# Where VectorE makes the token weights of a routed expert layer: early in its queue, or behind each tile's own gate product

## The chip, the cores and the metric

The kernel runs on one core of a Trainium2 chip, in float32 for everything that matters here. The metric is device microseconds (us) of one execution. The core has five engines with a queue each: TensorE (PE in the profile, its weight loads PEld), VectorE (DVE), ScalarE (ACT), GpSimd (POOL) and SyncE (SP). Each takes its instructions strictly in the order of its queue. DMAs are issued from SP's queue (plain ones) and from POOL's queue (indirect ones, which gather or scatter rows by a list of indices).

## The reference, cut to what matters

The program is a chain of four blocks over 2048 tokens of 128 features: an attention block with a gated feed-forward part, a routed expert layer (call it layer m), a slot-attention block, and a second routed expert layer (layer n). The change touches layer m alone:

```
shared_out = _expert(x, sg, su, sd)                 # silu(x @ sg.T) * (x @ su.T) @ sd.T
probs  = softmax(x @ wr.T + rb)                     # 7 routed experts
scores, idx = top_k(probs, 2);  scores = scores / scores.sum()
out = shared_out
for e in range(7):
    out = out + w[..., e:e + 1] * _expert(x, rg[e], ru[e], rd[e])   # w: scores at idx, else 0
```

So each token goes to two of seven experts, and each expert's result is multiplied by the token's weight for it, the "token weight" of the title.

## The kernel before, in words

Layer m sorts the 4096 pairs of token and expert by expert and cuts them into 38 tiles of at most 128 rows, one expert to a tile. Its steps, with the names and lines used below:

- **Shared expert.** `moe0_shared` (L1390) runs for four groups of 512 tokens. For each of three chunks it makes two products into PSUM (`gu`, L1397), a SiLU on ScalarE (`gss`, L1387) and the gate product on VectorE (`ma`, L1388); then 12 products, written as 24 matmuls in the profile, make `ym` (L603), and VectorE adds it to the residual `r` (L1402). `ym` lies in the pool `psX`, which has one buffer; the tiles' results `ynm` take the same buffer next, so the first tile cannot start before the last `r` addition has read `ym`.
- **Sorting.** `sort` (L1010) makes the lists: `frm` (which token rows a tile gathers), `to` (where its results go), and `sec` and `sgn` (L1105, L1106), which tell whether a row is its token's first or second choice. It also issues the first weight loads and gathers.
- **Gathers.** `fetch(j)` (L1257, DMA at L1264) gathers the 128 rows of tile j into `zs[j]`, each row 128 normalized features and one score. Two tiles share a buffer, and there are seven buffers, so 14 tiles fit. In the text F(j) is this gather on POOL's queue.
- **Weights.** `weights` (L1245, DMA at L1254, from SP's queue) loads the 576 KB of one tile's expert. There are six buffers; the load of tile j+6 waits for the last product of tile j.
- **Tile loop.** `tiles` (L1309). For tile j, TensorE does three gate products `gum` (L1410, six matmuls in the profile), the transposition of the next tile's rows (`turn`, L1316, copied to `zTn` by ScalarE at L1318), three more `gum`, and the down products of the tile before (`ynm`, L1421). ScalarE makes SiLU (`gsm`, L1387), VectorE the gate product (`am`, L1388), and ScalarE scales the result by the token weight on its way out of PSUM (`ysm`, L1425). `finish(j)` then issues the next weight load, the scatter of `ys` to `res` (L1325, R(j) in the text) and the next gather.
- **Token weight.** `moe0_down` (L1417) makes `wk[j]`, one number a row, from the score that came with the gather and from `sgn` and `sec` (L1419). It takes four buffers in turn, so wk(j) waits until `ysm` has used wk(j-4). It is also the last reader of `zs[j]` beside the transposition, so a gather into the same buffer waits for it.

The program is put in order by a scheduler that queues an instruction of an engine when it can be ready soonest by its own estimates; nothing in the source says where on VectorE's queue L1419 goes. As built, wk(0) stands in front of the addition of the third group's `ym`, wk(1), wk(2) and wk(3) stand behind it and in front of the last two `ma` of the shared expert, and from then on wk(j+4) stands between am(j+1) and am(j+2). On POOL's queue the built order is F(0) to F(15), R(0), then F F R R over and over, until the gathers are used up.

Of the kernel before, what the change touches and what calls it, by code (L numbers as in the profile page):

```python
# [15 lines left out]
ALU = mybir.AluOpType  # L16
# [5 lines left out]
D = 128  # L22
# [15 lines left out]
IP = 384  # L38
# [31 lines left out]
def pixart_kernel(  # L70
# [18 lines left out]
    V, S, G, PE = nc.vector, nc.scalar, nc.gpsimd, nc.tensor  # L89
# [768 lines left out]
    def wide(nm):  # L858
        return psS.tile([P, 512], F32, name=nm, tag="s")
# [524 lines left out]
    def silu_gate(a, gate, up, nm, n):  # L1384

        gs = ph.tile([P, 512], F32, name=f"gs{nm}", tag="gate2")[:, :n]
        S.activation(gs, gate, AF.Silu)  # L1387
        V.tensor_tensor(a, gs, up, ALU.mult)  # L1388

    def moe0_shared(R, i, zT):  # L1390
        g = R.b0 // 4 + i
        a = ph.tile([P, 3, 512], F32, name=f"ma{g}", tag="act")
        for c in range(3):
            ps = [wide(f"gu{g}_{c}_{j}") for j in range(2)]
            for j in range(2):
                w = j * IP + c * P
                PE.matmul(ps[j], lhsT=wsh[:, w : w + P], rhs=zT, start=True, stop=True)  # L1397
            silu_gate(a[:, c, :], ps[0], ps[1], f"s{g}_{c}", 512)
        y = psX.tile([P, 4, D], F32, name=f"ym{g}", tag="x")
        token_major(y, lambda c: a[:, c, :], lambda c: wsh[:, 2 * IP + c * D : 2 * IP + (c + 1) * D], 3)  # L1400
        rg = r[:, 4 * g : 4 * g + 4, :]
        V.tensor_tensor(rg, y, rg, ALU.add)  # L1402

    def moe0_up(w, zT, nm):
        ps = []
        for j in range(2):
            ps.append(wide(f"gu{nm}_{j}"))
            for c in range(3):
                k = j * IP + c * P
                PE.matmul(ps[j][:, c * P : (c + 1) * P], lhsT=w[:, k : k + P], rhs=zT, start=True, stop=True)  # L1410
            if j == 0:
                yield ps[0][:, IP:]
        a = ph.tile([P, IP], F32, name=f"a{nm}", tag="acts", bufs=3)
        silu_gate(a, ps[0][:, :IP], ps[1][:, :IP], nm, IP)
        yield a

    def moe0_down(w, a, y, ys, R, j):  # L1417
        wk = rt.tile([P, 1], F32, name=f"wk{j}", tag="wk", bufs=4)
        V.tensor_scalar(wk, R.zs[j][:, D : D + 1], R.sgn[:, j : j + 1], R.sec[:, j : j + 1], ALU.mult, ALU.add)  # L1419
        for c in range(3):  # L1420
            PE.matmul(  # L1421
                y, lhsT=a[:, c * P : (c + 1) * P], rhs=w[:, 2 * IP + c * D : 2 * IP + (c + 1) * D],
                start=(c == 0), stop=(c == 2),
            )
        S.activation(ys, y, AF.Copy, scale=wk)  # L1425
# [374 lines left out]
    for g in range(4):  # L1800
        moe0_shared(m0, g, zT[g])
    m0.tiles(moe0_up, moe0_down)
    slot_prologue()
    idle = wide("idle")
# [102 lines left out]
```

## Time and profile before

| | |
|---|---|
| time, median of 3 runs | 885.98 us (880.98 to 886.86) |
| the profiled execution | 882.33 us, of which span 880.6 us |
| mean granted TensorE clock | 0.955 of full speed |
| busy: PE, PEld | 783.8 us (89%), 623.0 us (71%) |
| busy: DVE, ACT, POOL | 548.8 us (62%), 411.7 us (47%), 358.9 us (41%) |
| moved by DMA | 65.18 MB, mean 74 GB/s |
| shared expert's last part and first gathers | about 484 to 507 us of the span |
| tile loop of layer m | about 507 to 614 us of the span |

Times in the views count from the first instruction of the span. In a timeline, a line gives start, duration, engine, source line, operation, output and inputs, how many instructions were merged, and in brackets how long the engine was idle before and what ended that. "issue" means that nothing the profile shows was waited for; "remote" that the wait was ended by something the profile cannot name. The ends of matmuls are modelled and not observed. POOL's rows for indirect DMAs show the issue, not the transfer.

### The profile page before, as it was taken

What the parts mean: (1) busy time and instruction counts of PE and PEld (TensorE: products, weight loads), DVE (VectorE), ACT (ScalarE), POOL (GpSimd) and SP (SyncE); (2) the same over time, 40 slices, a digit from 0 to 9 for tenths busy, and PEclk for the clock granted to TensorE, in tenths of its full rate; (3) what the DMA queues carried; (4) which work ended last, traced back from release to release, by engine and by line L of the source; (5) the groups of instructions that cost most, each with busy time, mean ns of one, the idle gap of its engine ahead of it and who ended that gap; (6) DMA issues with size and microseconds to landing.
All of it is one profiled execution on the core that took longest, in us unless ns stands there. A gap on an engine that the chain in (4) does not pass through costs nothing.

```text
span 880.6 us, 15517 instructions
## 1 busy us (share of the span) xinstructions
PE 783.8 (89%) x5469; PEld 623.0 (71%) x5469; DVE 548.8 (62%) x1748; ACT 411.7 (47%) x931; POOL 358.9 (41%) x457
## 2 busy tenths in 40 slices
PE   6999999999999999999899688789789898983776
PEld 4688887877678788765666478688476776673775
DVE  3687766765657776885879322232588799851333
ACT  3566767666654454443231023344486756231222
POOL 2234324241424333436430656654244445543565
PEclk9999999999999999999999889999989999956989
DMA  8200000001200000002002457774300000038873
GB/s 313 85 2 1 1 1 2 1 1 39 60 1 11 10 11 14 18 1 77 13 18 73 150 168 227 236 267 153 93 1 2 1 1 1 1 64 211 271 241 117
DMA packets 36529, 65.18 MB, mean 74 GB/s; under 512 B 4579, under 2 KB 25014, under 8 KB 35812
## 3 DMA queue, kind: packets, MB, share of 16 engines
q1 hardware_dynamic: 32179, 55.11, 20.4%
q0 software_dynamic: 4272, 9.09, 3.4%
q8 instruction: 43, 0.70, 0.3%
q14 instruction: 35, 0.28, 0.1%
HBM read 55.71 MB, written 8.93 MB: 73 GB/s over the span
## 4 chain that ended last, share of the span: by engine, by line
PE 73%; DVE 11%; issue 4%; ACT 4%; DMA 3%; POOL 3%; SPq 1%; another core or an unknown queue 1%; POOLq 0%; ACTq 0%; DVEq 0%
PE gum L1410 6%; PE pq L367 6%; PE ynm L1421 4%; PE pk L377 4%; PE te L524 3%; PE po L534 3%; PE s L471 3%; PE s L462 3%; PE ya L566 3%; PE pv L384 3%; PE pv L400 3%; PE ya L557 3%; PE h1n L1766 2%; PE idle L1526 2%; PE ynn L1776 2%
## 5 line engine op out<-in xcount | busy, mean ns | idle before, releaser
L509 POOL TENSOR_TENSOR e<-e,ri 128x1024 f32<-128x1024 f32 x32 | 61.0, 1909 | 143.4 <-DVE ri L495 130.3
L482 DVE TENSOR_REDUCE mx<-s 128x8 f32<-128x1024 f32 (+1 forms) x64 | 64.4, 1007 | 63.0 <-PE s L471 47.5
L494 DVE TENSOR_REDUCE ri<-e 128x8 f32<-128x1024 f32 (+1 forms) x64 | 63.7, 995 | 19.0 <-ACT e L490 18.3
L1410 PE MATMUL gum<-zTnm,wm 128*128 128x128 f32 x456 | 64.8, 285 | 11.8 <-ACT zTnm L1318 10.2
L503 POOL TENSOR_TENSOR es<-e,ri 128x512 f32<-128x512 f32 x64 | 43.4, 704 | 67.0 <-DVE ri L495 32.5
L367 PE MATMUL pq<-ha,wa 128*128 128x256 f32 x256 | 66.9, 397 | 2.9 <-ACT q L368 1.6
L1410 PEld LDWEIGHTS gum<-zTnm,wm 128*128 128x128 f32 x456 | 59.5, 200 | 13.5 <-ACT zTnm L1318 11.7
L487 DVE TENSOR_TENSOR e<-s,mx 128x1024 f32<-128x1024 f32 (+1 forms) x64 | 63.8, 997 | 2.0
L490 ACT ACTIVATE e<-e 128x1024 f32<-128x1024 f32 (+1 forms) x64 | 57.1, 892 | 5.9 <-DVE e L487 4.0
L1388 DVE TENSOR_TENSOR am<-gsm,gum 128x384 f32<-128x384 f32 x38 | 21.1, 554 | 55.7 <-ACT zTnm L1318 15.2
L1264 POOL DMA_INDIRECT zsm<-tok,frmm x38 | 36.8, 968 | 43.7 <-DVE row_latem L1099 20.2
L367 PEld LDWEIGHTS pq<-ha,wa 128*128 128x128 f32 x256 | 46.5, 199 | 10.5 <-ACT q L368 2.9
L1325 POOL DMA_INDIRECT res<-ysm,tom x38 | 37.3, 981 | 30.2 <-ACT ysm L1425 17.9
L377 PE MATMUL pk<-ctxT,wa 128*128 128x154 f32 x256 | 40.5, 295 | 0.6 <-ACT k L378 0.6
L524 PE MATMUL te<-ident,e 128*128 128x128 f32 x256 | 39.6, 277 | 0.0
L524 PEld LDWEIGHTS te<-ident,e 128*128 128x128 f32 x256 | 30.5, 141 | 12.1 <-issue 8.7
L471 PEld LDWEIGHTS s<-k,q 64*128 64x128 f32 x512 | 31.5, 191 | 10.3 <-issue 9.6
L525 ACT COPY eT<-te 128x512 f32<-128x512 f32 x64 | 37.8, 590 | 0.0
L1766 PE MATMUL h1n<-zTnn,wn 128*128 128x128 f32 x184 | 31.4, 306 | 6.2 <-issue 3.9
L1421 PE MATMUL ynm<-wm,am 128*128 128x128 f32 x228 | 33.0, 282 | 4.0 <-ACT ysm L1425 2.1
L471 PE MATMUL s<-k,q 64*128 64x128 f32 x512 | 34.6, 281 | 1.8 <-DVE e L487 1.8
L462 PE MATMUL s<-k,ha 128*128 128x308 f32 x128 | 36.1, 423 | 0.0
(437 smaller groups left out, 1987.6 us busy)
## 6 DMA issues: line engine op xcount, KB each, us to landing
wm<-in_moe_w_dram SPq DMA_DIRECT2D x38, 576.0 KB
wn<-in_moe_w_dram SPq DMA_DIRECT2D x23, 578.0 KB
wa<-in_attn_w_dram SPq DMA_DIRECT2D x4, 1024.0 KB
ygm<-res SPq DMA_DIRECT2D x8, 256.0 KB
vor<-vo SPq DMA_DIRECT2D x16, 104.0 KB
vr<-vor SPq DMA_DIRECT2D x8, 208.0 KB
tok<-stm SPq DMA_DIRECT2D x4, 258.0 KB
tok<-stn SPq DMA_DIRECT2D x4, 258.0 KB
```

Source lines behind the costliest of these rows:

```text
L367: PE.matmul(pq[:, j, :], lhsT=wqk[:, w : w + P], rhs=hT, start=True, stop=True)
L377: PE.matmul(pq[:, j, :], lhsT=wqk[:, w : w + D], rhs=kvT, start=True, stop=True)
L462: PE.matmul(ps[:, par, : 4 * nk].rearrange("p (j k) -> p j k", k=nk), lhsT=st["qT"][:, i * P : (i + 1) * P], rhs=st["kT"][:, h0 : h0 + 4, ...
L471: PE.matmul(ps[:, par, j * nk : (j + 1) * nk], lhsT=st["qT"][h0 : h0 + DH, c, i * P : (i + 1) * P], rhs=st["kT"][h0 : h0 + DH, c, i * nk : ...
L482: V.tensor_reduce(self.mx, self.ps, AX.X, ALU.max)
L487: V.tensor_tensor(self.e, self.ps, self.mx.unsqueeze(3).to_broadcast([P, 2, 4, nk]), ALU.subtract)
L490: S.activation(self.e, self.e, AF.Exp, scale=1.0 / math.sqrt(DH))
L494: V.tensor_reduce(self.ri, self.e, AX.X, ALU.add)
L509: G.tensor_tensor(self.e, self.e, self.ri.unsqueeze(3).to_broadcast([P, 2, 4, self.nk]), ALU.mult)
L524: PE.transpose(t[:nk, j, :], e[:, par, j, :], ident)
L1410: PE.matmul(ps[j][:, c * P : (c + 1) * P], lhsT=w[:, k : k + P], rhs=zT, start=True, stop=True)
L1421: PE.matmul(y, lhsT=a[:, c * P : (c + 1) * P], rhs=w[:, 2 * IP + c * D : 2 * IP + (c + 1) * D], start=(c == 0), stop=(c == 2),)
```

## The change

The gate product's instruction is kept in a list, and L1419 is traced inside `tc.issue_after(gated[j])`. That puts an edge of order, without a wait, between the two: on VectorE's queue wk(j) may not stand before am(j). Nothing is added to or taken from the work.

```
     def silu_gate(a, gate, up, nm, n):
         gs = ph.tile([P, 512], F32, name=f"gs{nm}", tag="gate2")[:, :n]
         S.activation(gs, gate, AF.Silu)
-        V.tensor_tensor(a, gs, up, ALU.mult)
+        return V.tensor_tensor(a, gs, up, ALU.mult).ins
...
+    gated = []
+
     def moe0_up(w, zT, nm):
...
-        silu_gate(a, ps[0][:, :IP], ps[1][:, :IP], nm, IP)
+        gated.append(silu_gate(a, ps[0][:, :IP], ps[1][:, :IP], nm, IP))
         yield a

     def moe0_down(w, a, y, ys, R, j):
         wk = rt.tile([P, 1], F32, name=f"wk{j}", tag="wk", bufs=4)
-        V.tensor_scalar(wk, R.zs[j][:, D : D + 1], R.sgn[:, j : j + 1], R.sec[:, j : j + 1], ALU.mult, ALU.add)
+        with tc.issue_after(gated[j]):
+            V.tensor_scalar(wk, R.zs[j][:, D : D + 1], R.sgn[:, j : j + 1], R.sec[:, j : j + 1], ALU.mult, ALU.add)
```

As built, the two programs have the same instructions. The queues of PE, ACT and SP are in the same order. Two queues differ:

```
VectorE before: ... ma wk0 r+=ym wk1 wk2 wk3 ma ma ... r+=ym ... am0 am1 wk4 am2 wk5 am3 wk6 ...
VectorE after:  ... ma r+=ym ma ma ... r+=ym ... am0 wk0 am1 wk1 am2 wk2 am3 wk3 am4 wk4 ...

POOL before: F0..F13 F14 F15 R0 F16 F17 R1 R2 F18 F19 R3 R4 F20 F21 R5 R6 ...
POOL after:  F0..F13 F14 R0 F15 R1 F16 R2 F17 R3 F18 R4 F19 R5 F20 R6 ...
```

So although the title speaks of the first tiles, the edge holds for all 38, and the order of gathers and scatters on POOL's queue changes with it.

## The prediction

> **What bounds the kernel now.** I read the chain of work that ended last, then VectorE's and TensorE's timelines where it leaves TensorE, then POOL's timeline and the clock of each stage in the tile loop. The chain, in order of time (start, duration, what):
>
> ```profile
> 493.44 4.19 issue
> 499.09 1.14 DVE zc L272 x4
> 500.23 5.84 another core or an unknown queue
> 507.64 1.64 PE gum L1410 x6
> ```
>
> Between the shared expert and the first `gum`, TensorE loses 4.19 us and then 5.84 us. VectorE's timeline says what stands in the first hole:
>
> ```profile
> 487.45 0.69 DVE L1388 TENSOR_TENSOR ma<-gss,gu 128x512 f32<-128x512 f32 x1 [1.52 <-PE gu L1397]
> 490.60 0.27 DVE L1419 TENSOR_SCALAR wk<-zsm,sgnm,secm 128x1 f32<-128x1 f32 x1 [2.46 <-DMA zsm<-tok,frmm]
> 490.79 0.68 DVE L1402 TENSOR_TENSOR r<-ym,r 128x512 f32<-128x512 f32 x1
> 493.40 0.27 DVE L1419 TENSOR_SCALAR wk<-zsm,sgnm,secm 128x1 f32<-128x1 f32 x1 [1.93 <-DMA zsm<-tok,frmm]
> 495.37 0.28 DVE L1419 TENSOR_SCALAR wk<-zsm,sgnm,secm 128x1 f32<-128x1 f32 x1 [1.70 <-DMA zsm<-tok,frmm]
> 496.70 0.27 DVE L1419 TENSOR_SCALAR wk<-zsm,sgnm,secm 128x1 f32<-128x1 f32 x1 [1.06 <-DMA zsm<-tok,frmm]
> 496.89 1.27 DVE L1388 TENSOR_TENSOR ma<-gss,gu 128x512 f32<-128x512 f32 x2
> ...
> 506.06 0.69 DVE L1402 TENSOR_TENSOR r<-ym,r 128x512 f32<-128x512 f32 x1 [5.82 <-remote]
> ```
>
> Four `wk` of 0.27 us wait for four gathers (2.46, 1.93, 1.70, 1.06 us), and the last two `ma` of the shared expert stand behind them until 496.89. TensorE waits with them:
>
> ```profile
> 493.06 0.38 PE L603 MATMUL ym<-wsh,ma 128*128 128x128 f32 x2
> 497.62 0.59 PE L603 MATMUL ym<-wsh,ma 128*128 128x128 f32 x2 [4.19 <-issue]
> 498.85 3.61 PE L603 MATMUL ym<-wsh,ma 128*128 128x128 f32 x20
> 506.80 0.48 PE L1316 MATMUL ynm<-ident,zsm 128*128 128x128 f32 x1 [3.90 <-DVE wvu L1505]
> ```
>
> The second hole is odd: `ym` ends at 502.46 on the page, but the addition that reads it starts at 506.06, 3.60 us later.
>
> In the tile loop POOL is nearly full while gathers last (40.90 of 64.40 us counted, and 0.30 us between issues besides). One turn of its queue for two tiles, F F R R:
>
> ```profile
> 546.85 0.98 POOL L1264 DMA_INDIRECT zsm<-tok,frmm  x1 [0.89 <-PE ynm L1421]
> 548.14 0.96 POOL L1264 DMA_INDIRECT zsm<-tok,frmm  x1 [0.30 <-issue]
> 549.41 1.00 POOL L1325 DMA_INDIRECT res<-ysm,tom  x1 [0.30 <-issue]
> 551.14 0.98 POOL L1325 DMA_INDIRECT res<-ysm,tom  x1 [0.73 <-issue]
> 553.00 0.98 POOL L1264 DMA_INDIRECT zsm<-tok,frmm  x1 [0.88 <-PE ynm L1421]
> ```
>
> A turn takes 553.00 - 546.85 = 6.15 us, 3.07 a tile. TensorE needs 2.12 us a tile (its starts once the gathers are over, after 582 us, are that far apart). And two stages (start and end, length, busy us of PE, PEld, DVE, ACT and POOL, then the granted clock, DMA share, GB/s):
>
> ```profile
> 497.90:501.20 3.30, 3.30 (x19) 3.30 (x19) 1.62 (x6) 0.00 (x0) 2.38 (x4) 0.50 0.22 58
> 516.90:581.30 64.40, 49.53 (x399) 46.90 (x398) 16.40 (x41) 19.52 (x61) 40.90 (x42) 0.97 0.75 236
> ```
>
> **The change part by part.** The sum starts from the profiled execution, 882.33 us (span 880.6); that is 3.65 under the median of the runs shown and inside their range.
>
> *A. The four waits in front of `ma`.* Without them the first of the two `ma` needs its SiLU (490.68 + 0.60) and a product whose matmuls end at 491.5; the second needs its SiLU (492.40 + 0.60 = 493.00) and a product that ends at 493.22. It would end at 493.3 + 0.68 = 494.0 instead of 498.16: **-4.2 us**.
>
> *B. The half clock behind the hole.* From 497.90 to 501.20 the clock is 0.50, and the 20 matmuls take 3.61 us; the 20 of the group before, at 487.14, took 2.64, most of them at full clock. From the end of `ma` to the end of `ym` before: 502.46 - 498.16 = 4.3 us. After: 494.0 to about 496.6, 2.6 us, if TensorE, busy from 487.7 on, keeps its clock: **-1.7 us**. If not, 0.
>
> [...]
>
> *C. The 3.60 us between `ym` on the page and its addition.* Nothing in the change touches it, and nothing on the page explains it. Last gathers were issued at 502.42. It may go with the hole, or stay. Bounds -3.6 and 0; I take the middle, **-1.8 us**.
>
> [...]
>
> A to C bring the first `ynm` transposition from 506.80 to 499.1. Its rows are there (the first gather landed before 490.60) and so are six tiles' weights (issued by 490.3). The weight load behind `ynm` of tile 0 on SP's queue moves along with it.
>
> *D. Gathers that are still on their way.* F(0) to F(13) leave POOL every 1.25 us until 503.36, whatever VectorE does; now tiles 0 and 1 run beside the last of them. Tiles 0 to 2 ran at 2.12 us in the trace, with two gathers beside them: 0. The other bound is what two gathers cost later, 6.15 - 2 x 2.12 = 1.9 us, for three pairs: +5.7. I take **+1**, nearer the row of these same tiles.
>
> *E. `wk` behind `am`, 38 times 0.27 us.* `ysm(j)` needs it, but `ynm(j)` must run in between: six matmuls of 0.83 us from when `am` ends. 0.5 us of cover remain: **0**; without the cover it would be 38 x 0.27 = 10 us. The waits of `wk` for `ysm` four tiles back (18 times, 11.2 us in all) disappear; `am` waited behind them, yet after nearly all of them it waited on for SiLU or for `gum`: 0.
>
> *F. POOL's queue.* F(14) and its successors now wait for `wk` of the buffer's second tile, one tile (2 to 3 us) later than for its transposition. The data have 14 tiles of lead, so no transposition waits. But R(0) stands behind F(14) and F(15) behind R(0), through all 24 remaining gathers. Lower bound: POOL without a wait, four issues of 1.28 us for two tiles, 2.56 a tile: 24 x (2.56 - 3.07) = -12.2. Upper bound: each pair waits for the whole chain, in which the second gather is issued 2.56 us after the first (a scatter stands between), 3.8 us pass until TensorE's results are through again (F at 540.54, next `ysm` at 544.34), and `am` and `wk` follow (0.9 us): 7.2 a pair against 6.15, 12 x 1.05 = +12.6. The nearest row is layer n's loop, which alternates R and F already: its down product starts at 824.9 for tile 5 and 869.6 for tile 19, 3.19 us a tile. I take that: 24 x (3.19 - 3.07) = **+2.9**. Gathers also end one or two tiles later, at about 1 us more each: **+1.4**.
>
> The sum: -4.2 - 1.7 - 1.8 + 1 + 2.9 + 1.4 = -2.4 us: 879.9 from the profiled execution, 883.6 from the median. Most of the runs shown lie nearer the median, but the sum is made on the execution. I say **880 us**.
>
> **The rivals.** *Forecast: the start is gained, the loop gives part of it back.* 880 us, own range 874 to 885.
>
> *Rival 1: POOL's alternation frees the loop.* With one gather at a time TensorE's results are held up less long, and the loop runs at POOL's own pace: start -7.7 + 1, loop -12.2 + 1.4 (the ending): -17.5, 865; half of the loop's gain gives 871. For it: R rows that alternate with nothing else, after 582 us, run without a lost us. Against: layer n alternates and is no faster.
>
> *Rival 2, the slower side: the longer chain from gather to gather decides.* Place: POOL's queue between F(15) and F(37), where each pair of gathers now hangs on `am` and `wk`. Price: +12.6, with +5.7 of D and the +1.4: from -7.7 to +12, so 894; it decides the sign once a pair takes more than 6.15 + 5.3/12 = 6.6 us (with D and the ending as I took them). For it: the turn of 6.15 us does start with a gather waiting for TensorE. Against: POOL works ahead of the data by many tiles and could let that chain slip.
>
> *Rival 3: the start isn't gained.* `ym` cannot finish before the last of F(0) to F(13) is through, as its end at 506 follows F(13) by 3.6 us; then the change gives 0 + 2.9 + 1.4, 887. For it: the 3.60 us of C. Against: `ma` and `gu` were read promptly at 490 to 499, amid the same gathers.
>
> **How the numbers follow.** Chances: forecast 0.54, rival 1 0.25, rival 2 0.09, rival 3 0.12. About 1%, 8.9 us, is what a measurement of this kernel can tell from no change: under 877.1 against the median is faster. Of the forecast a fifth lies below that, and a fifth of rival 1 above it; rival 3 falls within 1%; of rival 2 most is slower, and a little of rival 3. So faster 0.31, same 0.60, slower 0.09. The range reaches half into rival 1 and past rival 3: 869 to 889.
>
> **What would show it.** Right: no `wk` before 500 us, the two `ma` ended by about 494, no half clock at 497.9, the first transposition at 497 to 501, tiles about 3.1 us apart while gathers last. A: the 4.19 us hole gone from the chain. C: the distance from the last `ym` to its addition. F: the distance of gathers two apart on POOL; 5.1 us speaks for rival 1, over 6.6 for rival 2. Wrong: a first transposition still near 506 (rival 3), or `ysm` waiting for `wk` in VectorE's row (E).

## The result, and the profile after

| | before | after |
|---|---|---|
| median of 9 runs each, same chip | 885.98 us (880.98 to 889.28) | 893.71 us (889.46 to 898.55) |
| ratio after to before, 95% interval | | 1.0095 [1.0068, 1.0122] |
| the profiled execution, its span | 882.33, 880.6 us | 895.81, 894.1 us |
| first transposition (`ynm<-ident,zsm`) | 506.80 us | 506.22 us |
| loop of layer m, first to last `ysm` | 98.6 us | 108.3 us |
| from the last `ysm` to the end of the span | 268.6 us | 272.8 us |

Forecast were 880 us and a range of 869 to 889; the changed kernel takes 893.71, 1% more than the kernel before. One remark is needed to read everything below: the kernel before itself ran at two levels, at medians of 886 to 892 us in three sets of runs (this one among them) and of 850 to 854 us in four others, so each ratio is to runs of the kernel before on the same chip in the same set, and each experiment names that level (the text calls 886 to 892 us the upper one, 850 to 854 us the lower one).

VectorE's timeline of the changed kernel, in the stretch shown of the kernel before:

```profile
489.53 0.69 DVE L1402 TENSOR_TENSOR r<-ym,r 128x512 f32<-128x512 f32 x1 [1.73 <-issue]
491.31 0.69 DVE L1388 TENSOR_TENSOR ma<-gss,gu 128x512 f32<-128x512 f32 x1 [1.10 <-PE gu L1397]
493.03 0.69 DVE L1388 TENSOR_TENSOR ma<-gss,gu 128x512 f32<-128x512 f32 x1 [1.03 <-PE gu L1397]
...
505.48 0.69 DVE L1402 TENSOR_TENSOR r<-ym,r 128x512 f32<-128x512 f32 x1 [10.22 <-remote]
```

The four `wk` are gone and the last `ma` ends at 493.72 instead of 498.16. But the addition that ends the shared expert starts at 505.48 instead of 506.06. TensorE's timeline:

```profile
492.76 0.61 PE L603 MATMUL ym<-wsh,ma 128*128 128x128 f32 x4
493.77 2.50 PE L603 MATMUL ym<-wsh,ma 128*128 128x128 f32 x20
...
506.22 0.47 PE L1316 MATMUL ynm<-ident,zsm 128*128 128x128 f32 x1 [9.51 <-DVE wvu L1508]
```

The products follow at once and at full clock (1.00 granted from 493.77 to 496.27), and end at 496.27 on the page. Then comes a hole of 9.51 us that was 3.90 before. In the trace TensorE's next six signals all lie between 505.45 and 505.63: they were held. (Whether the products or only their signals were late the trace does not settle, since ends of matmuls are modelled. The clock speaks for the signals, if it falls behind an idle TensorE. That is the author's estimate from one place of the kernel before: it was granted at half from 497.88 us on, behind the hole at 493.44, in which TensorE had nothing to do. Here it was granted at half from 501.06 on, 4.4 us ahead of the signals, and in the kernel before once more from 504.71 on, 1.3 us ahead.) The windows that answer to those of before, with the clock in the third column from the end:

```profile
497.90:501.20 3.30, 0.00 (x0) 0.00 (x0) 0.00 (x0) 0.00 (x0) 2.39 (x4) 0.98 0.17 44
501.20:511.20 10.00, 4.98 (x23) 4.78 (x24) 2.67 (x9) 0.93 (x3) 1.56 (x2) 0.50 0.07 20
516.90:590.90 74.00, 55.75 (x416) 53.05 (x414) 16.27 (x44) 21.61 (x66) 43.59 (x45) 0.90 0.67 217
```

The half clock (0.50 in the second row) has moved behind the new hole, onto the first tiles. In the loop TensorE is busy for 55.75 of 74.00 us instead of 49.53 of 64.40. POOL's and ScalarE's timelines show one turn of it:

```profile
513.82 0.95 POOL L1264 DMA_INDIRECT zsm<-tok,frmm  x1 [10.76 <-PE gum L1316]
515.07 1.01 POOL L1325 DMA_INDIRECT res<-ysm,tom  x1 [0.30 <-issue]
516.39 0.98 POOL L1264 DMA_INDIRECT zsm<-tok,frmm  x1 [0.30 <-issue]
517.67 0.99 POOL L1325 DMA_INDIRECT res<-ysm,tom  x1 [0.30 <-issue]
518.97 0.97 POOL L1264 DMA_INDIRECT zsm<-tok,frmm  x1 [0.30 <-issue]
520.25 0.99 POOL L1325 DMA_INDIRECT res<-ysm,tom  x1 [0.30 <-issue]
521.54 0.97 POOL L1264 DMA_INDIRECT zsm<-tok,frmm  x1 [0.30 <-issue]
524.57 0.99 POOL L1325 DMA_INDIRECT res<-ysm,tom  x1 [2.06 <-DVE am L1388]
527.77 0.97 POOL L1264 DMA_INDIRECT zsm<-tok,frmm  x1 [2.21 <-PE ynm L1424]
```

```profile
515.06 0.37 ACT L1428 ACTIVATE ysm<-ynm,wk 128x128 f32<-128x128 f32 x1 [0.63 <-PE ynm L1424]
518.14 0.37 ACT L1428 ACTIVATE ysm<-ynm,wk 128x128 f32<-128x128 f32 x1 [1.57 <-PE gum L1316]
522.39 0.27 ACT L1318 COPY zTnm<-gum 128x128 f32<-128x128 f32 x1 [3.88 <-remote]
523.93 0.37 ACT L1428 ACTIVATE ysm<-ynm,wk 128x128 f32<-128x128 f32 x1 [0.88 <-remote]
```

POOL sends a gather every 2.57 us, with a scatter between, until it has run through the results it has (521.54). Meanwhile TensorE's results thin out: 515.06, then 518.14, then 523.93. They do not wait for the end of this stream, though: ScalarE reads the next one at 522.39, 3.4 us behind the gather at 518.97, but only 0.85 us behind the one at 521.54. Six intervals of over 4 us like this (5.79, 4.29, 6.51, 5.78, 7.21 and 4.05) stand in the loop, where before there were four, the longest 4.36.

### The profile page after: what moved, and what is told of

Its sections match the earlier page's. It is cut to its first block, busy times and chain, and to the rows that moved or that the text cites. A ratio compares the mean times of both kernels' runs of the same rounds, so it can differ in the third digit from the quotient of the medians.

```text
span 894.1 us, 15490 instructions
## 1 busy us (share of the span) xinstructions
PE 795.2 (89%) x5469; PEld 635.1 (71%) x5469; DVE 546.5 (61%) x1748; ACT 412.9 (46%) x931; POOL 359.8 (40%) x457
## 5 line engine op out<-in xcount | busy, mean ns | idle before, releaser
L1412 PE MATMUL gum<-zTnm,wm 128*128 128x128 f32 x456 | 69.8, 299 | 8.9 <-issue 7.2
L1412 PEld LDWEIGHTS gum<-zTnm,wm 128*128 128x128 f32 x456 | 64.4, 214 | 10.3 <-issue 7.9
L1325 POOL DMA_INDIRECT res<-ysm,tom x38 | 37.4, 984 | 31.8 <-ACT ysm L1428 16.8
L1424 PE MATMUL ynm<-wm,am 128*128 128x128 f32 x228 | 35.7, 297 | 9.3 <-ACT ysm L1428 8.0
L1424 PEld LDWEIGHTS ynm<-wm,am 128*128 128x128 f32 x228 | 31.4, 209 | 11.0 <-ACT ysm L1428 8.9
L1779 PE MATMUL ynn<-wn,an 128*128 128x128 f32 x184 | 28.2, 302 | 11.6 <-DVE ysn L1781 9.7
## 6 DMA issues: line engine op xcount, KB each, us to landing
wn<-in_moe_w_dram SPq DMA_DIRECT2D x23, 578.0 KB
```

The lines of the kernel that those rows point to most:

```text
L1424: PE.matmul(y, lhsT=a[:, c * P : (c + 1) * P], rhs=w[:, 2 * IP + c * D : 2 * IP + (c + 1) * D], start=(c == 0), stop=(c == 2),)
```

## The experiments

The first theory had two parts: TensorE's results are held until the first gathers are through, and POOL's alternation lengthens the loop; and what starts the holding is the fetch of a block of instructions that falls amid gathers, as one had come in each of the four longest stalls or just ahead of it (521.6, 547.7, 565.8 and 582.3 us). Such fetches are the transfers of the page's queue `q8 instruction`, 43 in the span; that they are TensorE's was the author's estimate. The rivals: the gathers alone hold the results, or the new place of `wk` costs. Four kernels, with the kernel before at 852 us:

**Edge for the first four `wk` only.** `with tc.issue_after(gated[j]) if j < 4 else ExitStack():`

> The edge is kept for wk(0) to wk(3) only; wk(4) and later stand on VectorE's queue where they stood before the change, and POOL's queue is back to F F R R from R(1) on. Theory 1 (the time is lost in the tile loop, by POOL's alternation of gathers and scatters; and the start gains nothing, because TensorE's results are held until the first fourteen gathers are through): first transposition near 506.2 us as in the changed kernel, loop of about 98.5 us from tile 0 to tile 37 as before, time 885 us (883 to 887). Rival (the early wk in front of ma were worth something to the start, and their removal alone costs): a loop as long as the changed kernel's 108 us, about 894 us.

Measured: 850.61 against 852.3 us, ratio 0.9975 [0.9943, 1.0007].

**Edge for all but the first four.** `with tc.issue_after(gated[j]) if j >= 4 else ExitStack():`

> The reverse: wk(0) to wk(3) stand early, in front of the last two ma of the shared expert, as before; the edge is kept for wk(4) to wk(37), and POOL alternates gather and scatter. Theory 1 (POOL's alternation costs in the loop): first transposition near 506.8 us, loop of 106 to 109 us, time 893 us (891 to 896). Rival (the removal of the early waits costs): 886 us.

Measured: 849.4 us, ratio 0.9968 [0.9935, 1.0001].

**The changed kernel, and the kernel before, with 128 instructions more on TensorE's queue at the start.** The pad is to bring the fetch at 495.2 us of the changed kernel (F(0) at 485.6) and the one at 498.5 us of the kernel before (F(0) at 485.9) ahead of the first gather.

```
+    pad = psM.tile([P, 2], F32, name="pad", tag="mm")
+    for _ in range(32):
+        PE.matmul(pad[:, 0:1], lhsT=ident, rhs=ident[:, 0:1], start=True, stop=True)
```

> The changed kernel with 32 products of one column added right behind the identity (128 more instructions on TensorE's queue, about 9 us before anything waits for them, which should be hidden at the start or cost under 2 us). [...] Theory 1 (TensorE's results are held when such a block is fetched while gathers are on their way): the addition of the last ym starts near 497 us instead of 505.5, the first transposition at 497.5, with the loop's stalls moved to other tiles: 885 us (880 to 890). Rival (the gathers alone hold the results, whatever is fetched): addition still at 505.5, time 894 us (892 to 896).

> The same 128 instructions added to the kernel before. Its fetch at 498.5 us moves to before the gathers too. Theory 1 (fetch amid gathers): the 3.6 us between the last ym and its addition vanish, first transposition near 503.2 us instead of 506.8, loop stalls at other tiles: 882 us (878 to 886). Rival (gathers alone): transposition still at 506.8 us, 886 us.

Measured: 859.26 us (1.0080 [1.0052, 1.0109]) and 864.44 us (1.0146 [1.0096, 1.0196]). The pad was not hidden: F(0) comes about 9 us later than in the two kernels above. All four told nothing about the theories, for a reason that none foresaw: nothing is held here. With the edge for four, the last addition starts at 496.35, 5.8 us ahead of F(13) on its way out (F(13) at 502.1), and tiles follow at 2.12 us; an instruction fetch at 494.9, amid gathers, did no harm there.

**Both kernels once more, unchanged,** for their traces beside each other at this level.

> The changed kernel itself, unchanged, once more. In the four runs just made, the kernel before took 852 us instead of 886, and in none of them were TensorE's results held in the first gathers. Theory 1b (the holding of TensorE's results belongs to the chip or its state in the first measurement, and the kernel's queues decide the time only where it happens): without the holding the changed kernel's first transposition is near 497 us, its tiles follow at 2.1 us, and its time is 848 to 851 us against 852 (ratio 0.995 to 1.000); with the holding it is again about 1.0095 times the kernel before. Rival (late token weights together with POOL's alternation hold the results on any chip): first transposition at 505 us again and ratio 1.01 even where the kernel before takes 852.

> The kernel before itself, for its profile beside the changed kernel's on the same chip. Theory 1b: where it takes 852 us, its first transposition is near 502.5 us instead of 506.8, since the addition of the last ym follows the last of its matmuls at once; tiles follow at 2.1 us until transfers are late; 852 us. Where it takes 886 us again, 506.8 us and pairs of 6.1 us again. Rival: 506.8 us in any case, and the 34 us come from elsewhere in the span.

Measured, kernel before at 853.65 us: the changed kernel 850.0 us, ratio 0.9947 [0.9920, 0.9973]; the kernel before against itself 0.9980 [0.9944, 1.0017], which says how much of such a ratio is noise. So here the change is no loss, but its gain is hardly clear of noise: the two medians measured side by side, 850.0 and 851.51 us, lie 1.5 us apart, and the two profiled executions, 851.61 and 848.22, lie the other way. The changed kernel's VectorE, TensorE, POOL, and a window of its loop:

```profile
496.53 0.69 DVE L1388 TENSOR_TENSOR ma<-gss,gu 128x512 f32<-128x512 f32 x1 [1.03 <-PE gu L1397]
499.81 0.69 DVE L1402 TENSOR_TENSOR r<-ym,r 128x512 f32<-128x512 f32 x1 [1.35 <-PE ym L603]
```

```profile
497.27 2.50 PE L603 MATMUL ym<-wsh,ma 128*128 128x128 f32 x20
500.55 0.33 PE L1316 MATMUL ynm<-ident,zsm 128*128 128x128 f32 x1 [0.34 <-DVE wvu L1508]
```

```profile
507.23 1.01 POOL L1325 DMA_INDIRECT res<-ysm,tom  x1 [0.30 <-issue]
508.55 0.97 POOL L1264 DMA_INDIRECT zsm<-tok,frmm  x1 [0.30 <-issue]
509.82 0.99 POOL L1325 DMA_INDIRECT res<-ysm,tom  x1 [0.30 <-ACT ysm L1428]
511.12 0.97 POOL L1264 DMA_INDIRECT zsm<-tok,frmm  x1 [0.30 <-PE gum L1412]
```

```profile
508.00:560.00 52.00, 51.86 (x458) 51.24 (x458) 17.76 (x48) 23.58 (x71) 39.50 (x42) 1.00 0.97 326
```

and the kernel before, the same place:

```profile
495.07 1.28 DVE L1388 TENSOR_TENSOR ma<-gss,gu 128x512 f32<-128x512 f32 x2
500.67 0.69 DVE L1402 TENSOR_TENSOR r<-ym,r 128x512 f32<-128x512 f32 x1 [2.79 <-PE ym L603]
```

Both additions follow the end of `ym` at once (0.04 and 0.03 us behind it on the page). POOL goes at 2.57 us a tile without a wait, with 0.30 us between issues, and TensorE is busy for 51.86 of 52.00 us. Counted from F(0) (488.2 and 484.6 us, a difference that arises far ahead of the change), the first transposition comes after 12.3 us instead of 16.8, and the last `ysm` after 98.5 instead of 101.0. 76 issues at 1.28 us (0.98 of issue and the 0.30 between) are 97.3 us: POOL's own pace by the author's estimate, which both kernels are close to.

The 34 us between the two levels arise only in stages with gathers. Matched instruction by instruction, the traces of the kernel before lie 1.3 to 2.3 us apart up to 499 us, 26 us apart at the end of layer m's loop, 23 us at the start of layer n's gathers, and 33 to 35 us at its end.

**Gathers as plain loads.** The next four ran at 892.35 us before, with results held.

```
+                if self.nk == 2 and j >= 14 and j % 2:      # second kernel: if self.nk == 2:
+                    dma(out=self.zs[j], in_=self.tok[j % 16 * P : (j % 16 + 1) * P, :])
+                    return
```

> The changed kernel, but twelve gathers of layer m (every second one from F(15) on) are plain loads from SyncE's queue of 128 consecutive rows: the same bytes from other rows, so those tiles compute with the wrong rows. POOL's queue loses 12 of 76 issues, the bytes stay. Theory 1b, where the kernel before takes 852 us: there the loop ends 98.5 us after F(0), and POOL alone needs 76 x 1.28 = 97.3 us for its issues; with 64 issues (82 us) TensorE's 2.12 us a tile decides, the last ysm comes 16.9 + 77.6 = 94.5 us after F(0), and the time is 846 us (844 to 848) against 850 for the changed kernel. Rival (the rate of the transfers, busy share 0.97 amid the loop, is what holds the loop): nothing changes, 850 us. Where the kernel before takes 886 us: start still held to 505 us, about half the long stalls gone, 884 to 890 us.

> The changed kernel with all 38 gathers of layer m as plain loads of consecutive rows from SyncE's queue (wrong rows, same bytes); only the scatters stay on POOL's queue. Where the kernel before takes 886 us this shows what the gathers do to TensorE's results: Theory 1b: no holding at the start (first transposition at about 497 to 500 us) and tiles at 2.12 us, layer m's loop 78 us instead of 108, time about 858 us (855 to 864); rival (something else in the stage holds the results): still 890 or more. Where the kernel before takes 852 us: loop 77.6 us, time 846 us (844 to 848).

Measured: 888.43 us (0.9963 [0.9934, 0.9992]) with twelve plain loads, 869.95 us (0.9765 [0.9712, 0.9819]) with all. With twelve the start is held as before (first transposition 20.9 us after F(0)) and two intervals of over 4 us are left of six. With none of layer m's gathers on POOL, VectorE shows the last addition 0.04 us behind the end of its products:

```profile
496.78 0.69 DVE L1391 TENSOR_TENSOR ma<-gss,gu 128x512 f32<-128x512 f32 x1 [1.03 <-PE gu L1400]
500.06 0.69 DVE L1405 TENSOR_TENSOR r<-ym,r 128x512 f32<-128x512 f32 x1 [1.35 <-PE ym L603]
```

and fourteen intervals in a row of 2.12 us, with the scatters still on POOL's queue. So here the gathers held the results, and the scatters alone did not. (The plain loads differ from gathers in two things, the queue and rows that lie side by side; which of them matters was not separated.) The expected 858 us were missed in the loop, 89.1 us instead of 78: the built order put products of the slot-attention block into it (`pwvu`, `pk` and others from 534.8 us on, and `pu` from 551.8 to 578.0 us, which the changed kernel runs from 626.8 to 636.8 us), and tiles then took 2.84 us. Why the time behind the loop, 275.4 us, is no shorter for it is not explained.

**Fewer gathers ahead.** `FETCH = 5`, and the same with ten instead of six `ysn` buffers.

> The changed kernel with five row buffers instead of seven, so that layer m issues ten gathers ahead instead of fourteen (layer n four instead of six). Where the kernel before takes 852 us: no holding at the start, POOL's issues are as many as before and alternate four tiles earlier: 850 us (849 to 854). Where it takes 886 us: if the results are held until the first stream of gathers is through, the last ym's addition comes four gathers (5 us) earlier, near 500.5 us, and the time is 889 (885 to 893); if the holding has nothing to do with the end of the stream, 505.5 and 894.

> As the run with five row buffers, and ten instead of six buffers for the tiles' results (ysm), so that ysm waits less for the scatter of the tile six back (5.7 us of ScalarE's idle time behind such waits in the changed kernel's loop, 10 times). If these waits are what stretches the loop where the kernel before takes 852 us: 846 to 847 us and no ysm waiting for a scatter; if POOL's issue rate is behind them (they only pass it on), 850 us as without. Where the kernel before takes 886 us: like the run with five row buffers within 1 us.

Measured: 924.51 us (1.0394 [1.0311, 1.0478]) and 924.84 us (1.0345 [1.0238, 1.0452]). The total misses by 35 us: layer n, with four gathers ahead, takes 306.2 us from the last `ysm` to the end instead of 272.8. The addition was met:

```profile
492.44 0.69 DVE L1388 TENSOR_TENSOR ma<-gss,gu 128x512 f32<-128x512 f32 x1 [1.03 <-PE gu L1397]
499.64 0.69 DVE L1402 TENSOR_TENSOR r<-ym,r 128x512 f32<-128x512 f32 x1 [3.17 <-remote]
```

Ten gathers, the last issued at 496.7: the results come 2.9 us later, as they came 3.4 us after the fourteenth. Both times the stream's end released them.

**The edge's halves, the pad, and the kernel before with plain loads,** now at 887.83 us before, held.

> The kernel of the first run (edge for wk(0) to wk(3) only) once more, to see it where TensorE's results are held, if this call meets that state: the kernel before at 885 to 892 us. Theory 2 (there TensorE's results and what hangs on them are held while POOL's first stream of gathers is on its way, so the start isn't gained; and in the loop one gather and one scatter in turn keep the holding up longer than two gathers and two scatters): start near 506 us, held to about 3 us after the last of the first gathers as in the changed kernel, tiles in pairs of 6.1 us as before; time equal to the kernel before within 0.5%. Rival (the token weights' new place costs, not POOL's order): 1% slower, like the changed kernel. Where the kernel before takes 852 us: 0.9975 again.

> The kernel of the second run (edge for wk(4) and later, POOL alternating) once more, for the same reason. Where the kernel before takes 885 to 892 us, theory 2: start as before, loop of 104 to 109 us, 1% slower (ratio 1.007 to 1.012). Rival: equal to the kernel before. Where the kernel before takes 852 us: 0.997 again.

> The changed kernel with 128 more instructions on TensorE's queue at the very start, once more. On the other occasion these cost 9.2 us by themselves, and put TensorE's instruction fetch 6 us ahead of the first gather instead of 10 us behind it. Where the kernel before takes 885 to 892 us: theory 1 (the holding starts with an instruction fetch that falls amid gathers) has the last ym added as soon as its products are through, 16 us before the loop's first ysm no longer but 11 us after F(0), and a ratio to the kernel before of 1.00 or less; theory 2 (the gathers alone) has it held until 3 us after F(13), 20 us after F(0), as in the changed kernel, and a ratio of 1.02 (the changed kernel's 1.0095 and the 9.2 us of the pad). Where the kernel before takes 852 us: 1.008 again.

> The kernel before with all 38 gathers of layer m as plain loads of consecutive rows from SyncE's queue (wrong rows, same bytes), as was done with the changed kernel, which then took 0.9765 of the kernel before's time, there 892 us, with nothing held at the start. Theory 2 (without POOL's gathers the change gains its start, A and B, 5 to 6 us, and nothing is given back in the loop): this kernel is 3 to 6 us slower than the changed kernel so altered, 0.981 to 0.984 of the kernel before's time. Rival (the early wk cost the start nothing once gathers are out of the way): the same as it, 0.9765.

Measured: 890.84 us (1.0037 [1.0006, 1.0068]), 892.2 us (1.0060 [1.0033, 1.0088]), 901.17 us (1.0164 [1.0111, 1.0217]), 863.93 us (0.9774 [0.9711, 0.9837]).

- The pad ends the theory of the instruction fetch. Fetches lie at 489.9 and 528.3, gathers from 495.6 to 512.1, and VectorE still shows

```profile
504.23 0.69 DVE L1391 TENSOR_TENSOR ma<-gss,gu 128x512 f32<-128x512 f32 x1 [1.03 <-PE gu L1400]
515.55 0.69 DVE L1405 TENSOR_TENSOR r<-ym,r 128x512 f32<-128x512 f32 x1 [8.13 <-remote]
```

  The first kernel of this section, with a fetch at 494.9 us and tiles at 2.12 us behind it, agrees.
- At the upper level the start went with the gathers alone. From F(0) to the first transposition it is 20.9 us in the kernel before and 20.7 in the changed kernel, with either half of the edge, and with the pad. At the lower level it is 16.6 to 18.4 us in five runs with early `wk` and 11.4 to 12.4 in five without.
- Each half of the edge has a cost in the loop. From F(0) to the last `ysm` it is 126.1 us before, 130.4 and 130.5 with one half, 135.7 with both. That each costs half is not shown: the changed kernel with the pad, whose POOL, VectorE and ScalarE keep the changed kernel's order, took 131.4, so one trace is good to some 4 us only. POOL's timeline with the first half (F(16) to F(19)):

```profile
516.16 0.99 POOL L1325 DMA_INDIRECT res<-ysm,tom  x1 [0.30 <-issue]
517.45 0.97 POOL L1264 DMA_INDIRECT zsm<-tok,frmm  x1 [0.30 <-issue]
518.72 0.99 POOL L1325 DMA_INDIRECT res<-ysm,tom  x1 [0.30 <-issue]
520.01 0.97 POOL L1264 DMA_INDIRECT zsm<-tok,frmm  x1 [0.30 <-issue]
521.88 0.94 POOL L1264 DMA_INDIRECT zsm<-tok,frmm  x1 [0.90 <-remote]
523.13 0.95 POOL L1264 DMA_INDIRECT zsm<-tok,frmm  x1 [0.30 <-issue]
525.89 0.99 POOL L1325 DMA_INDIRECT res<-ysm,tom  x1 [1.81 <-ACT zTnm L1318]
```

  Here four gathers alternate with scatters, and with the last of them begins the loop's longest interval, 7.18 us (`ysm` at 518.1 and 525.3), in which F(17), F(18) and F(19) follow each other without a scatter, so it is not the work of alternation alone; from F(18) on they come in pairs, and no interval is over 4.7 us. That kernel was expected to equal the kernel before; the four alternating gathers had been overlooked.
- Without gathers on POOL the kernel before is as fast as the changed one: the rows are there early, its four `wk` run at 486.6 without a wait, and the last two `ma` wait for their own products alone. The expected difference of 3 to 6 us isn't there. What A removed is the wait for gathers, not the `wk`. The loops are alike too, 89.3 and 89.1 us, with tiles at 2.12 us in both until the slot-attention products come, although `wk` stands early in one and behind `am` in the other. So the new place of `wk` costs nothing by itself; it costs only with gathers on POOL's queue.

**One queue at a time.** The changed kernel with gathers in pairs on POOL, and the kernel before with the changed kernel's order on POOL; all other queues are untouched.

```
+                put.append(scat.ins)                        # scat: the scatter of finish(j)
+                with tc.issue_after(put[j - 1]) if j % 2 == 0 and j >= 2 else ExitStack():   # pairs, on after
+                with tc.issue_after(put[j - 3]) if j >= 3 else ExitStack():                  # alternating, on before
                     self.fetch(j + self.ahead)
```

> The changed kernel with one more edge: the gather of an even tile stands behind the scatter of the odd tile before it on POOL's queue, which makes the queue F14 R0 R1 F15 F16 R2 R3 F17 F18 and so on; VectorE's, ScalarE's, TensorE's and SyncE's queues stay as the change left them. Theory 2 (where TensorE's results are held, the kernel before at 885 to 892 us, POOL's one-by-one alternation keeps a gather on its way all the time; pairs leave a gap behind each second gather): loop of 98 to 101 us instead of 108, no stall over 5.5 us in the loop, ratio to the kernel before 0.997 to 1.002. Rival (wk behind am on VectorE's queue lengthens the loop): 1.0095 as the changed kernel. Where the kernel before takes 852 us: 0.994 to 0.998 by either.

> The reverse: the kernel before, token weights early as they were, with an edge that puts each gather from F(15) on behind a scatter, so that POOL's queue is exactly that of the changed kernel (F14 R0 F15 R1 F16 R2 ...) and all other queues are those of the kernel before. Theory 2, where TensorE's results are held: start near 506.8 us as before, loop of 106 to 110 us with stalls of 6 to 7 us, ratio 1.008 to 1.013. Rival: equal to the kernel before. Where the kernel before takes 852 us: 0.996 to 1.000 by either.

> The changed kernel with gathers in pairs on POOL's queue, once more, for the state in which TensorE's results are held (last time the kernel before took 850 us, and the ratio was 0.9991). There, theory 2: loop of 98 to 101 us, no stall over 5.5 us, ratio 0.997 to 1.002; rival (wk behind am lengthens the loop): 1.0095. Where the kernel before takes 852 us again: 0.999 again.

> The kernel before with the changed kernel's order on POOL's queue alone, once more (last time the kernel before took 850 us, and the ratio was 1.0000). Where TensorE's results are held, theory 2: start near 506.8 us, loop of 106 to 110 us, stalls of 6 to 7 us, ratio 1.008 to 1.013; rival: equal to the kernel before. Where the kernel before takes 852 us again: 1.000 again.

Measured: both times the kernel before ran at the lower level (850.39 and 853.58 us), where nothing is held. Pairs 0.9991 [0.9962, 1.0020] and 0.9959 [0.9935, 0.9982]; alternating 1.0000 [0.9973, 1.0026] and 0.9970 [0.9941, 0.9999]. POOL's order alone is worth nothing that can be told from noise there. Inconclusive for the question asked.

## Why the prediction was wrong

- **A** was right: the last `ma` ended at 493.72 (forecast 494.0).
- **B** was right in place: from the end of `ma` to the end of `ym` on the page 2.55 us (2.6). But the half clock came back behind the next hole: the row 501.20:511.20 has 0.50, behind 9.51 us of idle.
- **C is the step that failed.** "Nothing in the change touches it" was wrong: the delay is not a piece behind `ym` of its own length, it lasted until the first stream of gathers was through, 3.4 us behind F(13) here and 2.9 us behind the tenth where only ten were issued. It grew from 3.6 to 9.2 us and ate A and B. The start gained 0.58 us instead of 7.7. This is rival 3 in its own words, given 0.12 (its 887 us lacked the loop's loss); "read promptly at 490 to 499, amid the same gathers" was put against it, and is true up to 493.0 in the changed kernel; it says nothing of what came behind.
- **D and F** together were mis-sized: 5.3 us forecast, +9.7 measured in the loop. F's bounds (-12.2 and +12.6) held it. Gathers two apart on POOL are 6.52 us from F(15) to F(37) on average, against 6.15 and close to the 6.6 of rival 2. But it is not rival 2's chain from gather to gather: gathers went out at 2.57 us until POOL had no results left to scatter (521.54), and around that time TensorE's results came through (522.39). Layer n's 3.19 us a tile was the wrong row to take: the two levels differ by 10 to 12 us in its gathers, so it had the same holding built in, with other work around it.
- **E** was right: in the whole loop of the changed kernel 1.6 us are waited for `wk` (POOL 0.7 and 0.3, TensorE 0.6), and each `wk` ended at least 0.87 us before the later of the two other things that its `ysm` stood behind, the end of `ynm` on the page and ScalarE's instruction before it.
- The rest, +4.2 us behind layer m, is not explained by a step; the profiled execution of before lies 3.65 us under its median, and other runs at that level have 271.8 to 276.4 us there, the kernel before's 268.6 being the shortest. So the medians' 7.7 us, not the 13.5 of the two profiles, is the change.

At the lower level the forecast's own story happened: the start gained 4.5 us (B 1.7 of it: from the last `ma` to the end of `ym` 2.55 instead of 4.29), and the loop gave 2.0 back. The ratio of 0.9947 would be 4.5 us in all, more than these 2.5 and within the noise of them. What the loop gave back went to POOL's pace, which rival 1 had named; but the kernel before goes at that pace there too, so rival 1's 12 us aren't to be had.

**What stays open.** What sets the level: a chip of the same number showed both, and the rows compared don't tell them apart ahead of the first gathers. And whether, where results are held, it is POOL's alternation that lengthens the loop. The 1.6 us of waits for `wk`, the equal loops without gathers on POOL, and the pace of gathers speak for it. From F(19) to F(37) gathers two apart are 6.42, 6.64 and 6.76 us on average in the three kernels that alternate there (the changed one, the same with the pad, the second half of the edge), and 6.18 and 6.38 in the two with pairs (the kernel before, the first half): the order is right, but the gap is thin. And in those runs VectorE's order, and with it the moment at which `wk` lets each gather go, changed in the same place, and the two kernels that change one queue alone did not meet the level. No version was found that beats both kernels at both levels by more than the noise.

## What to carry to other kernels

When an addition starts microseconds after the product that it reads has ended on the page, look for what else ends at that moment, and count the delay as lasting until then: removing work ahead of it brought the start 0.58 us here, of 7.7 forecast. When an edge of order on one engine frees a buffer later, write out what the scheduler does to every queue that waits for the buffer, and price that against a trace in which the same holding is present or absent, not against one that has it built in. And run the kernel before again beside each experiment: with two levels 4% apart, a change was 1% slower at one and no slower at the other.

## What the runs showed of the hardware

TensorE's results were held while a stream of gathers from POOL's queue was on its way, and this was seen only at the upper of two levels of the same program: behind the first stream they were released 2.9 to 3.6 us after the last gather's issue there, and at once (0.03 to 0.04 us behind the product's end on the page) at the lower one. VectorE's signals were not held with them: in the changed kernel the last `ma` ended at 493.72 us and TensorE used it at 493.77. With plain loads of as many bytes from SyncE's queue in place of the gathers, and the scatters still on POOL's, nothing was held: the addition came 0.04 us behind the product's end in both kernels, at that same upper level.

The record of signals has gaps at the upper level, so a count of it shows nothing about delays here. The trace of before holds 1464 records for VectorE's 1508 signals and 730 for ScalarE's 783, against 1510 and 784 records at the lower level, and 2167 records of landings against 3973, for 36529 and 36528 packets. None of VectorE's and ScalarE's missing records lies ahead of the first gathers, and that `ma` has none, although TensorE acted on it at once.
